# A perceiver block on one core: the last group's self attention on float32 weights, and Mamba's buffers handed to the last stage

## The chip, the cores and the metric

The kernel runs on one core of a Trainium2 chip. The metric is the device time of one execution in microseconds; lower is better. A kernel's time is the median of several executions, and one more execution is recorded with the hardware profiler.

## The reference, cut to what matters

Eight batches of 64 query rows (512 wide) pass through six residual layers. The change touches layer 5, and its buffers touch layer 2.

```python
x = x + xattn0(layernorm(x), ctx, ...)   # cross attention, 32 heads, 1601 context rows
x = x + mamba(layernorm(x), ...)         # selective scan, 1024 channels x 16 states
x = x + ternary_ffn(layernorm(x), ...)
x = x + xattn1(layernorm(x), ctx)        # attention on the raw context, no weights
x = x + attention_fwd(layernorm(x), wq, wk, wv, wo)   # causal, 32 heads of 16
x = x + octonion_ffn(layernorm(x), w_gate, w_up, w_down)

def attention_fwd(x, wq, wk, wv, wo):
    xq, xk, xv = heads(x @ wq.T), heads(x @ wk.T), heads(x @ wv.T)   # 512 x 512 each
    xq, xk = rotary(xq), rotary(xk)
    probs = softmax(where(causal, xq . xk * 0.25, -1e30))
    return (probs . xv) @ wo.T
```

## The kernel before, in words

The first cross attention is the long part: for each batch and each of eight KV heads it projects keys and values, scores, exponentiates and sums. The layers after it work on a "group" of two batches, 128 rows, in a generator called `chain`. There are four groups. The chains of the first three are drawn out under the cross attention of later batches: `advance` takes steps from them by a clock of planned costs (`SPAN`, `CHAIN_COST`). When the last batch's cross attention is done, the fourth chain starts with nothing left to hide under, and the third chain is not yet finished. From about 2430 us to the end these two chains run side by side. In this text they are the **third group** and the **last group**. The order of the instructions on each engine is fixed when the program is built, by a scheduler that works with planned times; on the chip every engine takes its instructions in that order.

Weights come from DRAM at every use. A weight product goes through `mm3`: the left side and the weight are each held as a high and a low float32r part, and three matmuls (high x high, high x low, low x high) make one product of 128 x 512. The parts of the four 512 x 512 attention weights are made once, early, by `prep`, and kept in DRAM as `wat_s` (the profile's `d_wat`); the float32 originals are the input `attnT`. Where a weight is exact in one part (`exact=True`: the ternary layers, `d_ffn`, `d_gu`, `d_dn`), two matmuls are enough.

All loads are issued by one queue, SP's, in program order, so a load that waits for its buffer holds those behind it. Buffers are taken from pools by tag, with a number of slots for each tag:

- The last group draws from the pool `tp` with `BUFS_TAIL`: `s4` (slots of 4 KB in each partition) holds Mamba's inputs and scan tiles, the high and low weight pair of an `mm3` (tile `s`), the context tiles of the second cross attention and the gate and up weights `gu`; `w2` (slots of 2 KB, 12 of them, tile `w`) holds Mamba's projection weights, the ternary weights and the down weights `dn`.
- The third group holds its weights in tile `w_r`: 4 slots of 2 KB, `REST = {"w2": 4}`. Its attention loads high and low parts one by one.
- The first three groups have one pool, `cp`, for all other tiles, Mamba's among them (`a2`, `lv`, `bc`, `xpad`, `sm`).

In the last group's `attn1`, the projections for K, Q and V come in this order, then scores and values for four blocks of eight heads (`scores`, `values`), and the output product `wo` block by block. `ffn1` follows with an order of its own (`FFN_TAIL`): `lins` (gate and up, matmuls of L1200, one block of 48), `act` and `down`. In the third group `ffn1` takes its steps one after another: for each of three column ranges (512, 512, 336) gate, up, `act`, `down`. It has two PSUM buffers, and `dn` keeps one of them to the end. The lines of the steps: L740, L742 and L743 are the three matmuls of `mm3`; L699 transposes a normalised row block, L1095 a rotated K or Q, L1152 the probabilities, L1223 the input of `down`; L1118 puts the causal mask into PSUM (a float32 matmul), L1125 scores, L1159 values; L101 and L102 make the high and low part of a left side; L1086 is the rotation's first step; L1204 takes gate or up out of PSUM; L714 to L717 with L127 to L130 are the silu; L1235 is the last addition, L771 stores the output.

Of the kernel before, what the change touches and what calls it, by code (L numbers as in the profile page):

```python
# [9 lines left out]
FR = mybir.dt.float32r  # L10
# [6 lines left out]
P = 128  # L17
D = 512
NC = 4
# [21 lines left out]
AVPLAN = ((), (), (0, 1, 2, 3), (4, 5, 6, 7), (8, 9, 10, 11), (12,))  # L41
EXPLAN = ((0,), (1, 2), (3,), (4, 5), (6,), ())
BUFS = {"a2": 4, "lv": 3, "bc": 1, "xpad": 1, "b2": 5, "b4": 2, "w2": 3, "xr": 2}
BUFS_TAIL = {"a2": 6, "du": 2, "bc": 2, "xpad": 4, "s4": 10, "kb": 3, "b2": 8, "b4": 3, "w2": 12, "xr": 2}

# [28 lines left out]
class Kernel:  # L76
# [11 lines left out]

    def sb(self, tag, shape, dt=FP, bufs=None, pool=None):
        if pool is None:  # L90
            pool, bufs = self.cp, bufs or self.bufs.get(tag)
            if tag in REST and self.tp and not self.tail:
                pool, bufs, tag = self.tp, REST[tag], tag + "_r"
        return pool.tile(shape, dt, name=self.nm(tag), tag=tag, bufs=bufs)
# [624 lines left out]
    def lin(self, lt, wts, N=D, exact=False, tg="w2"):  # L719
# [3 lines left out]
            self.mm3(ps, lambda a: lt(c, a), w, N, c == 0, c == len(wts) - 1, exact, tg)  # L723
        return ps

    def mm3(self, ps, lhsT, wt, N, start, stop, exact=False, tg="w2"):

        nc = self.nc
        if exact:
            wh = self.sb(tg, [P, D], FR)[:, :N]  # L730
            nc.sync.dma_start(out=wh.bitcast(FP), in_=wt)
        elif self.tail:
            w = self.sb(tg, [P, 2, D], FR)
            nc.sync.dma_start(out=w.bitcast(FP), in_=wt)
            wh, wl = w[:, 0], w[:, 1]
        else:
            wh, wl = (self.sb(tg, [P, D], FR) for _ in range(2))
            nc.sync.dma_start(out=wh.bitcast(FP), in_=wt[:, 0])
            nc.sync.dma_start(out=wl.bitcast(FP), in_=wt[:, 1])
        nc.tensor.matmul(ps, lhsT=lhsT(0), rhs=wh, start=start, stop=False)  # L740
        if not exact:
            nc.tensor.matmul(ps, lhsT=lhsT(0), rhs=wl, start=False, stop=False)  # L742
        nc.tensor.matmul(ps, lhsT=lhsT(1), rhs=wh, start=False, stop=stop)  # L743
# [334 lines left out]

    def attn1(self, x, xo):
        nc = self.nc  # L1080
        lt = self.lnT(x, P)
        tr = []
        for m in (1, 0):
            ps = self.lin(lt, self.wat_s[m], tg=self.t4)
            t1 = self.sb("b2", [P, D])
            nc.scalar.activation(t1, ps, AF.Copy, scale=self.rot[:, 0:1])  # L1086
            r = self.sb("b2", [P, D])
            psv = ps.rearrange("p (d two) -> p d two", two=2)
            tv = t1.rearrange("p (d two) -> p d two", two=2)
            rv = r.rearrange("p (d two) -> p d two", two=2)  # L1090
            nc.vector.scalar_tensor_tensor(rv[:, :, 0], psv[:, :, 1], self.rot[:, 1:2], tv[:, :, 0], ALU.mult, ALU.add)
            nc.vector.scalar_tensor_tensor(rv[:, :, 1], psv[:, :, 0], self.rot[:, 2:3], tv[:, :, 1], ALU.mult, ALU.add)
            tp = self.acc().rearrange("p (c t) -> p c t", t=P)
            for c in range(NC):
                nc.tensor.transpose(tp[:, c, :], r[:, c * P : (c + 1) * P], self.ident)  # L1095
            t = self.sb(self.tl, [P, NC, P])
            nc.scalar.copy(t, tp)
            tr.append(t)
            yield 4
        kT, qT = tr  # L1100
        ps = self.lin(lt, self.wat_s[2], tg=self.t4)

        vb = self.sb("b4", [P, 16, 2, 32])
        nc.gpsimd.memset(vb, 0.0)
# [4 lines left out]
                    ps[k * T : (k + 1) * T].rearrange("p (hp h2 d) -> p hp h2 d", h2=2, d=16)[:, :, h2, :],  # L1109
                )  # L1110
        yield 4
        ot = self.sb("b4", [P, 2, NC, P], FR)

        def scores(c):
            sp = self.acc()
# [31 lines left out]
        def values(c, s):  # L1147

            tp = self.acc().rearrange("p (k q) -> p k q", q=P)
            sf = s.rearrange("p h t -> p (h t)")  # L1150
            for k in range(NC):
                nc.tensor.transpose(tp[:, k, :], sf[:, k * P : (k + 1) * P], self.ident)  # L1152
            pT = self.sb("b2", [P, NC, P])
            nc.scalar.copy(pT, tp)
            op = self.acc()
            for b in range(2):
                cols = slice(b * T, (b + 1) * T)
                for k in range(NC):
                    nc.tensor.matmul(op[k * 32 : (k + 1) * 32, cols], lhsT=vb[:, c * NC + k, b, :], rhs=pT[:, k, cols], start=True, stop=True)  # L1159
            self.split(ot[:, 0, c], ot[:, 1, c], op[:, :P])  # L1160

        def wo(c):
            self.mm3(ps, lambda a: ot[:, a, c], self.wat_s[3][c], D, c == 0, c == NC - 1, tg=self.t4)

        ahead = self.ahead
        ss = []
        for c in range(NC + ahead):
# [3 lines left out]
            if c >= ahead:  # L1171
                values(c - ahead, ss[c - ahead])
                yield 3
                if self.tail:
                    if c == ahead:
                        ps = self.acc()
# [64 lines left out]
    def run(self):  # L1241
        nc, tc, ctx = self.nc, self.tc, self.ctx
        nc.scalar.preload_act_table_set("natural_log_exp_and_others")
        self.setup(bufs=BUFS, accb=2, hs=4, tail=False, ahead=1, **TAGS)
        self.pc = ctx.enter_context(tc.tile_pool(name="pc", bufs=2, space=PSUM))
        xctx = ctx.enter_context(ExitStack())
        self.px = xctx.enter_context(tc.tile_pool(name="px", bufs=2, space=PSUM))
        self.consts()
        self.scratch()
        self.xw = ctx.enter_context(tc.tile_pool(name="xw", bufs=2))  # L1250
        self.xp = xctx.enter_context(tc.tile_pool(name="xp", bufs=2))
        qctx = ctx.enter_context(ExitStack())
        self.q_ln(qctx.enter_context(tc.tile_pool(name="qp", bufs=2, side="right")))
        B = self.B
        sizes = GROUPS.get(B) or [1] * B
        groups, k = [], 0
        for m in sizes:
            groups.append(list(range(k, k + m)))
            k += m
        self.place = {b: (k * T, len(g) * T) for g in groups for k, b in enumerate(g)}  # L1260
        side, self.tp = [], None

        def start(gen, now, cost, end):
            env = {k: getattr(self, k) for k in ENV}
            if not self.tail:
                env["nc"] = Side(self, PINNED)
            side.append({"gen": gen, "cost": cost, "got": 0.0, "t0": now, "end": end, "env": env})

        def advance(now):
            base = {k: getattr(self, k, None) for k in ENV}  # L1270
            for c in list(side):
                self.setup(**c["env"])
                goal = c["cost"] * min(1.0, (now - c["t0"]) / max(c["end"] - c["t0"], 1e-9))
                if now >= c["end"]:
                    goal = 1e9
                while c["got"] < goal:
                    try:
                        c["got"] += next(c["gen"])
                    except StopIteration:
                        if PRINT_COST:  # L1280
                            print("side", c["got"])
                        side.remove(c)
                        break
            self.setup(**base)

        gi, now, xdone = 0, 0.0, 0.0
        for cost, fin in self.x_all(list(range(B))):
            xdone += cost
            advance(xdone / X_COST)
            if fin == 0:  # L1290
                qctx.close()
                self.cp = ctx.enter_context(tc.tile_pool(name="cp", bufs=2, side="right"))
                start(self.prep(), xdone / X_COST, PREP_COST, PREP_END)
            if fin is not None and gi < len(groups) and groups[gi][-1] == fin:
                g = groups[gi]
                now = xdone / X_COST
                last = gi == len(groups) - 1
                if last:
                    self.pinning = False
                    xctx.close()  # L1300
                    self.pc = ctx.enter_context(tc.tile_pool(name="pt", bufs=3, space=PSUM))
                    self.cp = self.tp = ctx.enter_context(tc.tile_pool(name="tp", bufs=2))
                    self.setup(bufs=BUFS_TAIL, accb=6, hs=8, tail=True, ahead=2, **TAGS_TAIL)
                start(self.chain(gi, g), now, CHAIN_COST, now + SPAN[gi])
                if last:
                    side.insert(0, side.pop())
                gi += 1
        while side:
            now += 0.01
            advance(now)  # L1310
# [1 line left out]

TAGS = {"tw": "a2", "ts": "a2", "td": "a2", "tc4": "b4", "tk": "b2", "t4": "w2", "tl": "b2", "tn": "w2", "tv": "lv"}
TAGS_TAIL = {"tw": "w2", "ts": "s4", "td": "s4", "tc4": "s4", "tk": "kb", "t4": "s4", "tl": "s4", "tn": "w2", "tv": "s4"}
ENV = ("nc", "cp", "pc", "bufs", "accb", "hs", "tail", "ahead", *TAGS)
GROUPS = {8: [2, 2, 2, 2], 2: [2]}
SPAN = [3.1,3.1,2.6,0.2]
PREP_END = 2.8
FFN_TAIL = (("l", 0), ("l", 1), ("a", 0), ("l", 2), ("a", 1), ("d", 0), ("a", 2), ("d", 1), ("d", 2))
REST = {"w2":4}  # L1320
OTB = 1
SPV, HV = 2, 1
X_COST = 236.0
# [112 lines left out]
```

## Time and profile before

| | |
|---|---|
| median of 3 executions | 2746.58 us (2745.26 to 2748.1) |
| profiled execution: device time | 2747.45 us |
| profiled execution: span of the trace | 2745.6 us |
| instructions | 47783 |
| third group's Mamba layer done (last L743 on tile `a`) | about 2400 us |
| third and last group alone on the core | about 2430 to 2745.6 us |
| HBM traffic | 384.42 MB read, 72.48 MB written |

The profiled execution is 1.85 us longer than its span, which is what lies around the trace, and 0.87 us above the median.

How to read the views: the page gives busy time by engine and, in 40 slices of 68.6 us, the busy share in tenths. The chain of waits follows the work that ended last back to what released it; each line has start, length in us, and what it was: an engine's instruction, or a DMA waited for. The timeline lists the instructions of an engine in order of time; a bracket gives the idle time before one and what ended it. SPq is the DMA queue; its lines give when loads were issued. Instructions named f32 on TensorE include float32r; a true float32 matmul shows as two instructions.

### The profile page before, as it was taken

Reading aid. Unit: us, or ns where it says so; the run is one execution under the profiler, and the core shown is the slowest. Engines: PE = TensorE matmul, PEld = TensorE weight load, DVE = VectorE, ACT = ScalarE, POOL = GpSimd, SP = SyncE. Lnnn points to the kernel's source line nnn. Section 1 sums busy time; section 2 is a strip of 40 time slices with the busy share of each in tenths; the row PEclk is TensorE's granted clock in tenths of the full one; section 3 lists DMA queues with packets and bytes.
Section 4 is the critical chain, followed back from the end, with each engine's and each line's share of the span. In section 5 each row is a group of like instructions: output and inputs, shape, how many; then the busy total and the mean of one; then the engine's idle time right before and its main releaser. Section 6 shows DMA issues by size and latency. Waiting matters only on the chain.

```text
span 2745.6 us, 47783 instructions
## 1 busy us (share of the span) xinstructions
PE 2584.6 (94%) x17840; PEld 2303.7 (84%) x17840; DVE 1756.7 (64%) x2988; ACT 1378.4 (50%) x3318; POOL 1163.1 (42%) x1175
## 2 busy tenths in 40 slices
PE   7999999999999899999999989999999999976778
PEld 6999999889889899978988988988897998954545
DVE  4544345577777886545587787454668787549645
ACT  4444555444556554544456555444556555435433
POOL 3212444474579653421367344421348435215220
PEclk9999999999999999999999999999999999978889
DMA  9544446664666234664325534665333543465676
GB/s 305 151 144 152 131 155 221 204 205 156 212 208 212 71 116 164 215 192 155 114 78 156 156 106 131 199 203 165 125 101 97 168 153 126 146 221 197 219 253 218
DMA packets 312167, 460.03 MB, mean 168 GB/s; under 512 B 81272, under 2 KB 188792, under 8 KB 307456
## 3 DMA queue, kind: packets, MB, share of 16 engines
q1 hardware_dynamic: 311936, 456.99, 51.6%
q8 instruction: 140, 2.29, 0.3%
q14 instruction: 91, 0.75, 0.1%
HBM read 384.42 MB, written 72.48 MB: 166 GB/s over the span
## 4 chain that ended last, share of the span: by engine, by line
PE 60%; DVE 15%; DMA 9%; POOL 7%; issue 5%; ACT 4%; SPq 1%; POOLq 0%; DVEq 0%; ACTq 0%
PE v_ps L325 14%; PE k_ps L354 13%; PE o_ps L438 8%; PE s_ps L374 7%; DVE a L62 4%; PE w_ps L495 3%; POOL a L62 3%; PE acc L270 2%; POOL ss L426 2%; PE acc L1000 2%; PE acc L1053 2%; PE acc L740 2%; DMA cst<-in_ctxT_dram 2%; PE acc L743 1%; PE acc L785 1%
## 5 line engine op out<-in xcount | busy, mean ns | idle before, releaser
L354 PE MATMUL k_ps<-cxb,wk 128*128 128x256 f32 x3840 | 560.9, 291 | 21.8 <-ACT cxb L101 9.6
L354 PEld LDWEIGHTS k_ps<-cxb,wk 128*128 128x128 f32 x3840 | 504.9, 191 | 55.8 <-issue 15.1
L325 PE MATMUL v_ps<-wv,cxb 128*128 128x256 f32 x3840 | 521.5, 283 | 7.4 <-DVE mx L381 3.3
L325 PEld LDWEIGHTS v_ps<-wv,cxb 128*128 128x128 f32 x3840 | 479.2, 189 | 28.2 <-issue 13.9
L374 PE MATMUL s_ps<-q,kt 128*128 128x256 f32 (+1 forms) x2496 | 414.9, 299 | 13.3 <-DVE kt L105 4.9
L438 PE MATMUL o_ps<-S,v 128*128 128x256 f32 (+1 forms) x1664 | 409.2, 380 | 1.7 <-ACT S L416 1.6
L374 PEld LDWEIGHTS s_ps<-q,kt 128*128 128x128 f32 (+1 forms) x2496 | 339.7, 185 | 38.0 <-DVE kt L105 7.2
L381 DVE TENSOR_TENSOR mx<-s_ps,mx 128x512 f32<-128x512 f32 x256 | 175.3, 685 | 306.5 <-ACT S L377 306.3
L426 POOL TENSOR_TENSOR ss<-ss,S 128x512 f32<-128x512 f32 x256 | 355.0, 1387 | 16.2 <-ACT S L416 1.5
L377 ACT COPY S<-s_ps 128x512 f32<-128x512 f32 (+1 forms) x448 | 241.5, 551 | 211.8 <-PE s_ps L374 210.7
L438 PEld LDWEIGHTS o_ps<-S,v 128*128 128x128 f32 (+1 forms) x1664 | 296.4, 190 | 33.9 <-ACT S L416 2.5
L418 POOL TENSOR_TENSOR ss<-S,S 128x512 f32<-128x512 f32 x64 | 84.2, 1316 | 566.2 <-ACT S L416 566.0
L104 ACT ACTIVATE kt<-k_ps,c_bk 128x256 fp32r<-128x256 f32 (+1 forms) x384 | 184.7, 481 | 220.1 <-PE k_ps L354 216.1
L105 DVE SCALAR_TENSOR_TENSOR kt<-k_ps,c_bk,kt 128x256 fp32r<-128x256 f32 (+1 forms) x384 | 187.7, 489 | 144.0 <-ACT kt L104 143.2
L415 DVE TENSOR_TENSOR S<-S,m_ps 128x512 f32<-128x512 f32 (+1 forms) x448 | 257.6, 641 | 28.6 <-PE m_ps L401 27.6
L416 ACT ACTIVATE S<-S 128x512 f32<-128x512 f32 (+1 forms) x448 | 247.2, 599 | 42.5 <-DVE S L415 41.9
L328 ACT COPY v<-v_ps 128x256 f32<-128x256 f32 (+1 forms) x416 | 152.3, 367 | 219.6 <-PE v_ps L325 217.9
L62 ACT ACTIVATE a<-lv,c_A_log 128x128 f32<-128x128 f32 x384 | 122.7, 392 | 126.6 <-DVE lv L62 120.3
L62 POOL TENSOR_TENSOR a<-bc,lv 128x512 f32<-128x512 f32 x96 | 128.2, 1336 | 127.7 <-DVE a L62 112.4
L102 POOL TENSOR_TENSOR cxb<-cst,cxb 128x256 fp32r<-128x256 f32 x160 | 126.3, 804 | 120.9 <-ACT cxb L101 118.0
L62 DVE TENSOR_TENSOR_SCAN a<-a,a 128x512 f32<-128x512 f32 x96 | 145.1, 1512 | 48.3 <-POOL a L62 47.9
L325 PE MATMUL v_ps<-wv,cxt 128*128 128x256 f32 (+1 forms) x1152 | 161.8, 286 | 2.2 <-DVE kt L105 2.2
(348 smaller groups left out, 3972.0 us busy)
## 6 DMA issues: line engine op xcount, KB each, us to landing
wo<-d_wo SPq DMA_DIRECT2D x96, 512.0 KB, 4.9
wk<-d_wk SPq DMA_DIRECT2D x63, 512.0 KB, 3.4
wv<-d_wv SPq DMA_DIRECT2D x31, 1024.0 KB, 7.0
cst<-in_ctxT_dram SPq DMA_DIRECT2D x160, 128.0 KB, 3.1
b<-in_ctxN_dram SPq DMA_DIRECT2D x36, 512.0 KB, 4.2
d_q<-q_t SPq DMA_DIRECT2D x32, 512.0 KB, 4.3
q<-d_q SPq DMA_DIRECT2D x64, 256.0 KB, 3.6
d_wo<-b SPq DMA_DIRECT2D x32, 512.0 KB, 2.9
```

The source lines that it names most:

```text
L62: return lambda *a, **k: self.tc.keep_in_program_order(f(*a, **k))
L104: nc.scalar.activation(hi, src, AF.Identity, bias=bias)
L105: eng.scalar_tensor_tensor(lo, src, bias, hi.bitcast(FP), ALU.add, ALU.subtract)
L325: nc.tensor.matmul(ps[:r], lhsT=cx[:, a, c, o : o + r], rhs=w[:, m, c, :], start=k == 0, stop=k == 11)
L354: nc.tensor.matmul(ps[:, :wd], lhsT=w[:, a, c, :], rhs=cx[:, m, c, :], start=k == 0, stop=k == 11)
L374: nc.tensor.matmul(sp[:r, gi, :], lhsT=kt[:, a, u * P : u * P + r], rhs=q[:, m, :], start=k == 0, stop=k == 2)
L377: nc.scalar.copy(s[:r, :n], sp[:r, :n])
L381: nc.vector.tensor_tensor(mx, sp, S[0] if len(S) == 1 else mx, ALU.max)
L415: nc.vector.tensor_tensor(sv, sv, ps[:r, 1:2].to_broadcast([r, w, 256]), ALU.add)
L416: nc.scalar.activation(sv, sv, AF.Exp, scale=ISC)
L426: nc.gpsimd.tensor_tensor(ss, ss, S[n], ALU.add)
L438: nc.tensor.matmul(ps[:, 0], lhsT=self.v[(b, j, t)][:r, hc : hc + P], rhs=S[t // 2][:r, t % 2], start=t == 0, stop=t == NT - 1)
```

## The change

1. In the last group, `attn1` takes its left sides as one float32 tile (`lnT` with `hl=False`, `ot` without a low part) and its weights as float32 from `attnT`, in a new function `mm32`: one load of 256 KB into a slot of `w2` and one float32 matmul for each product, in place of one load of 512 KB into a slot of `s4` and three float32r matmuls. There are 16 such products: K, Q, V and `wo`, four each.
2. Mamba's tags move from `cp` to a pool `ca` of their own, stacked on `cp`. When the last group starts, `ca` is closed together with the cross attention's pool, and `tp` may use its memory.
3. `s4` gets 16 slots in place of 10.

The third group's attention stays as it is.

```diff
-BUFS_TAIL = {"a2": 6, "du": 2, "bc": 2, "xpad": 4, "s4": 10, "kb": 3, "b2": 8, "b4": 3, "w2": 12, "xr": 2}
+BUFS_TAIL = {"a2": 6, "du": 2, "bc": 2, "xpad": 4, "s4": 16, "kb": 3, "b2": 8, "b4": 3, "w2": 12, "xr": 2}
...
-            pool, bufs = self.cp, bufs or self.bufs.get(tag)
+            pool, bufs = self.ca if tag in MAMBA_TAGS else self.cp, bufs or self.bufs.get(tag)
...
+    def mm32(self, ps, x, wt, start, stop):
+
+        w = self.sb("w2", [P, D])
+        self.nc.sync.dma_start(out=w, in_=wt)
+        self.nc.tensor.matmul(ps, lhsT=x, rhs=w, start=start, stop=stop)
...
     def attn1(self, x, xo):
         nc = self.nc
-        lt = self.lnT(x, P)
+        tail = self.tail
+        lt = self.lnT(x, P, hl=not tail)
+        w32 = self.i["attnT"]
+
+        def proj(m):
+            if not tail:
+                return self.lin(lt, self.wat_s[m], tg=self.t4)
+            ps = self.acc()
+            for c in range(NC):
+                self.mm32(ps, lt(c, 0), w32[m, c], c == 0, c == NC - 1)
+            return ps
...
-        ot = self.sb("b4", [P, 2, NC, P], FR)
+        ot = self.sb("b4", [P, 1, NC, P]) if tail else self.sb("b4", [P, 2, NC, P], FR)
...
-            self.split(ot[:, 0, c], ot[:, 1, c], op[:, :P])
+            if tail:
+                nc.scalar.copy(ot[:, 0, c], op[:, :P])
+            else:
+                self.split(ot[:, 0, c], ot[:, 1, c], op[:, :P])
...
+            if tail:
+                self.mm32(ps, ot[:, 0, c], w32[3, c], c == 0, c == NC - 1)
+            else:
+                self.mm3(ps, lambda a: ot[:, a, c], self.wat_s[3][c], D, c == 0, c == NC - 1, tg=self.t4)
...
+                actx = ctx.enter_context(ExitStack())
+                self.ca = actx.enter_context(tc.tile_pool(name="ca", bufs=2, side="right"))
...
                     xctx.close()
+                    actx.close()
...
-                    self.cp = self.tp = ctx.enter_context(tc.tile_pool(name="tp", bufs=2))
+                    self.ca = self.cp = self.tp = ctx.enter_context(tc.tile_pool(name="tp", bufs=2))
...
+MAMBA_TAGS = ("a2", "lv", "bc", "xpad", "sm")
```

More of the change, by code (lines that the diff above doesn't have):

```diff
@@ L1080, in attn1 @@
         nc = self.nc
-        lt = self.lnT(x, P)
+        tail = self.tail
[8 more added lines that the diff above has]
+            return ps
         tr = []
         for m in (1, 0):
-            ps = self.lin(lt, self.wat_s[m], tg=self.t4)
+            ps = proj(m)
             t1 = self.sb("b2", [P, D])
@@ L1100, in attn1 @@
         kT, qT = tr
-        ps = self.lin(lt, self.wat_s[2], tg=self.t4)
+        ps = proj(2)
         vb = self.sb("b4", [P, 16, 2, 32])
@@ L1159, in values @@
                     nc.tensor.matmul(op[k * 32 : (k + 1) * 32, cols], lhsT=vb[:, c * NC + k, b, :], rhs=pT[:, k, cols], start=True, stop=True)
-            self.split(ot[:, 0, c], ot[:, 1, c], op[:, :P])
+            if tail:
+                nc.scalar.copy(ot[:, 0, c], op[:, :P])
+            else:
+                self.split(ot[:, 0, c], ot[:, 1, c], op[:, :P])
         def wo(c):
-            self.mm3(ps, lambda a: ot[:, a, c], self.wat_s[3][c], D, c == 0, c == NC - 1, tg=self.t4)
+            if tail:
+                self.mm32(ps, ot[:, 0, c], w32[3, c], c == 0, c == NC - 1)
+            else:
+                self.mm3(ps, lambda a: ot[:, a, c], self.wat_s[3][c], D, c == 0, c == NC - 1, tg=self.t4)
         ahead = self.ahead
@@ L1314 @@
 TAGS_TAIL = {"tw": "w2", "ts": "s4", "td": "s4", "tc4": "s4", "tk": "kb", "t4": "s4", "tl": "s4", "tn": "w2", "tv": "s4"}
-ENV = ("nc", "cp", "pc", "bufs", "accb", "hs", "tail", "ahead", *TAGS)
+ENV = ("nc", "cp", "ca", "pc", "bufs", "accb", "hs", "tail", "ahead", *TAGS)
 GROUPS = {8: [2, 2, 2, 2], 2: [2]}
```

## The prediction

> **What bounds the kernel now.** First the page, for the place. TensorE is busy 94% of the span at a full clock; the last five slices (2402 us on) are another regime: PE falls to 6 or 7 tenths, the clock to 7 or 8, DMA rises to 7.
>
> ```profile
> PE   7999999999999899999999989999999999976778
> PEclk9999999999999999999999999999999999978889
> DMA  9544446664666234664325534665333543465676
> ```
>
> Only there does the change act: no engine's order differs before the last group's Mamba scans. So next the chain of waits from 2640 us (start, length, what).
>
> ```profile
> 2655.25 5.94 DMA s<-d_wat
> ...
> 2661.24 0.79 PE acc L740
> 2662.03 0.43 PE acc L742
> ...
> 2672.29 5.37 DMA s<-d_wat
> ...
> 2679.36 1.71 PE acc L1118 x2
> ...
> 2694.44 0.86 PE acc L1118 x2
> ...
> 2709.97 8.96 PE acc L1200 x31
> ```
>
> The last group's Q and V weights arrive late (5.94 and 5.37 us), and after each wait TensorE runs at half clock: a 128x512 float32r matmul takes 0.43 us, later 0.23; the float32 mask matmul 1.71, later 0.86. Then comes the block of L1200. Last, the timeline of TensorE after it: the third group ends the kernel, not the last group.
>
> ```profile
> 2721.52 0.60 PE L1223 MATMUL acc<-ident,b 128*128 128x128 f32 x4
> 2723.77 0.49 PE L740 MATMUL acc<-w_r,b 128*128 128x512 f32 x1 [1.65 <-ACT b L101]
> ...
> 2727.63 0.39 PE L740 MATMUL acc<-w_r,b 128*128 128x336 f32 x1 [1.12 <-DMA w_r<-d_gu]
> ...
> 2739.83 0.49 PE L740 MATMUL acc<-w_r,b 128*128 128x512 f32 x1 [0.57 <-ACT b L101]
> ```
>
> These are the third group's second down-projection (to 2726.5), its last gate and up (to 2733.4) and its third down-projection (to 2741.9). Both groups finish within 3 us of each other, so a gain for one is worth only what the other allows.
>
> **What the Trainium skill says.** "TensorE: Matmul & The Clock Gate", What's actually happening: the clock is half after an idle window of about 3.4 us, full after as long a busy one. The trace agrees: 0.43 against 0.23 us. The same page's opening table calls the queues of ScalarE and VectorE strict FIFO; agrees: at 2578.74 ScalarE did the third group's L1086 (0.69 us) before the last Mamba cast L101 at 2579.32, which TensorE waited for. "FP8 and Floating Point Precision", TensorE Precision Notes: true FP32 takes four passes; agrees: 0.86 is 3.7 times 0.23. "DMA: Bandwidth & Descriptors", Anatomy of one DMA, gives 2.0 us plus bytes at 436 GB/s for GpSimd's path, an estimate of 2.6 us for 256 KB; SP's loads of that size, four alone at 2648.5, had a median of 2.5 us, the fourth 3.95.
>
> **The change part by part**, set against the span (2745.6).
>
> *Costed at nothing.* The pools: the third group's Mamba is done at 2400, and `tp`'s first load waits for the cross attention's pool anyway (issued 2429.72). Should `ca` be freed late, that load and all behind it on SP move by as much. Mamba with 16 slots: SP waited 19.3 + 6.2 us at L734 for slots, and these waits shrink, but VectorE is busy 48.4 of 50 us in 2500 to 2550, so the scans set the pace. The down weights: eleven loads of 256 KB stood before attention in the queue or within it; eight `attnT` loads of the same size take eight of those places, and `dn` follows the attention's weights. Its cover is the whole score stage, over 20 us. Traffic falls by 16 x 0.26 = 4.2 MB, 14 us of DMA at the 300 GB/s of 2650 to 2710; after 2710 DMA is 34% busy, so this shortens waits only where I count them below.
>
> *To the last group's K* (2649.5 before). Taken: 2.5 us earlier. The Mamba cast now stands ahead of L1086 and the third group's matmuls around it come later (2 us at the last L743), and the left side has no low part (L102, 0.7). Against it, eleven context loads now stand in SP's queue ahead of the third group's K weights c2 and c3, and those matmuls stand in TensorE's order ahead of the last Mamba L743; Q c2, loaded behind four `attnT` loads, stands ahead of the last group's scores. Bounds: 5 us earlier, 6 later. K starts at 2647.
>
> *K to the L1200 block* (60.5 us before: 2649.5 to 2709.97).
> - The weight waits go: 5.9 + 5.4. The slow matmuls behind them go: eleven float32r by 0.20, three by 0.20, L1118 and the scores after it by 1.8, together 4.6. Two waits for `w_r` on a loaded DMA (0.5 each) go. Sum -16.9.
> - Sixteen products: 0.86 for 3 x 0.23: +2.7. Four passes aside, K starts after 7 us with little work, so two of its matmuls at half clock: +1.7.
> - TensorE's new order: two of the third group's `wo` products (0.7 each) move behind K, +1.4; 16 of its gate and up matmuls leave, 16 x 0.23 = -3.7; scores of blocks 1 and 2 lose their overlapped partner, a lone one taking 1.0 us, +1.5; its first gate matmul stands between these scores and must wait until L102 frees one of two PSUM buffers, +1.5.
> - VectorE's new order puts the third group's silu (L715, L129, L130, L717, four times 0.7) between the steps of the layer norm ahead of the block: +2.8.
>
> Sum 51.5, so the block starts at 2698.5. It takes its 11.5 us as before (the idle stretch before it, and so the half clock, is alike) and ends at 2710.0, **11.5 us earlier** than 2721.5.
>
> *After the block* (24.1 us before). Here the third group has more left. Before, its second gate and up came before the block; now they follow it. Gate: weights there, 8 x 0.23 = 1.9. Up: its four loads take the slots that gate frees; SP issues 0.55 apart, the fourth lands 3.95 later: done at +6.1. Then the order has two of the last group's down-projections (transposes 0.6, cast 0.58, subtraction 0.69, hops, eight matmuls 1.9) and only then the transposes of the third group's second one. These wait for its silu, and VectorE has 11 us of work from +7 on: two silus of the last group, one of the third (3.6), two subtractions. Transposes at +17.5, second down-projection done at +21.9 with 14 matmuls shared. From there as before (2726.5 to 2745.6): four slots, two rounds of loads, silu, last down-projection, 19.1. Sum 41.0, which is 16.9 more than before.
>
> The end is at 2710.0 + 41.0 = 2751.0; some 40 hops of 0.02 to 0.05 us ("issue" in the chain) are not in the sum, +1. So 2752.0, **6.4 us more** than 2745.6. Against the median 2746.58, which stands 0.87 below the profiled 2747.45: **2753 us**.
>
> **The rivals.** The forecast's own range is 2748 to 2760.
> (a) *The saved waits carry through.* For it: 11.3 us of waits on the chain are certain to go, and with the clock kept full and the silu clear of the layer norm the block would end at 2704 (less 1.7, 2.8 and 1.5). If what follows then costs 33.5 us (24.1 as before, 6.1 for gate and up, 3.3 for the down-projections between), the end is 2737.5 on the span's clock, against the median 2738.5. Against it: four slots, one load round each 4 us. It decides as soon as the block ends more than 17 us earlier, or what follows costs under 5 us more than before.
> (b) *A head-of-queue wait on the way to K.* The eleven context loads are 5.4 MB; at 330 GB/s 16 us. If they are not landed by 2578, the third group's K c2 holds the last Mamba product and all behind it: 4 to 10 us, 2760 with the rest as forecast. For it: SP's in-order queue. Against: DMA runs at 133 GB/s in 2560 to 2570, so there is room.
> (c) *Gain and loss cancel.* If the terms of order (+1.5, +1.5, +2.8) hide beside other work, the end is 2747.
> That the change does not do what it says is excluded: the built order shows 16 loads from `attnT` and 16 single products on `w`.
>
> **How the numbers follow.** A measurement here can tell about 0.2% (5.5 us: 2741.1 to 2752.1) from no change. Forecast 0.53, of which 0.16 falls below 2752.1; (a) 0.22, nearly all faster; (b) 0.12, slower; (c) 0.13, same. Faster 0.21, same 0.30, slower 0.49. For 8 in 10, leaving out half of (a)'s lower side and (b)'s upper end: 2738 to 2766.
>
> **What would show it.** Right: no wait for `d_wat` by the last group; the L1200 block ends 9 to 14 us earlier; at the end SP issues some 26 `w_r` loads in rounds of four, and the last group's store stands well before the third's. Wrong: a block that ends under 6 us earlier (the terms of order or (b) are larger), or a third group whose last gate starts before 2725 (then (a)).

## The result and the profile after

The changed kernel takes 2764.59 us (median of 4, 2761.38 to 2772.36), the kernel before 2745.92 in the same comparison: ratio 1.0064, 95% interval 1.0049 to 1.008. The profiled execution took 2765.68 us, its span 2763.8, which is 18.2 more than before.

The page first: engine and DMA rows by slice.

```profile
PE   7999999999999899999999989999999999977886
PEclk9999999999999999999999999999999999977898
DMA  9544446664665244764325533655323553375753
```

The last five slices are again the only odd ones (TensorE 7, 7, 8, 8, 6 tenths where it was 7, 6, 7, 7, 8). The chain of waits from 2575 us (start, length, what), of the changed kernel:

```profile
2586.03 5.42 DMA w_r<-d_wat
...
2659.86 4.84 PE acc L730 x8
...
2667.08 3.45 PE acc L730 x8
...
2672.86 3.44 PE acc L730 x8
...
2711.10 9.90 PE acc L1223 x48
2721.50 3.33 DMA w_r<-d_gu
...
2742.90 3.48 DMA w_r<-d_gu
```

K, Q and V of the last group (L730, three times eight instructions, two to a float32 product) no longer wait for weights; 3.44 us for eight is 0.86 for a product, and K's 4.84 holds the slow clock. Both waits for `d_wat` are gone. The block (L1223, L1200 before) ends at 2721.0, where it ended at 2721.7 before: by the two traces' own clocks 0.7 us is left of what was saved (how much of that is scatter follows below). And after it come two waits for the third group's weights. TensorE's timeline there (a bracket is the idle time and what ended it):

```profile
2724.96 0.47 PE L746 MATMUL acc<-w_r,b 128*128 128x512 f32 x1 [2.10 <-DMA w_r<-d_gu]
...
2742.51 0.39 PE L749 MATMUL acc<-w_r,b 128*128 128x512 f32 x1
2743.94 0.39 PE L746 MATMUL acc<-w_r,b 128*128 128x336 f32 x1 [1.04 <-DMA w_r<-d_gu]
...
2755.51 0.88 PE L1246 MATMUL acc<-ident,b 128*128 128x128 f32 x3 [4.66 <-DVE b L1236]
```

These are the third group's second up projection, the last product of its second down-projection, its last gate, and the transposes of its third down-projection, which wait 4.66 us for its silu. The store of the last group's output is issued at 2742.4, the third's at 2760.9.

So that runs can be compared, the time is cut into stages, each read from the timelines: the end of the cross attention's output (L495, nothing of the change acts ahead of it); from there to the last group's K; K to the block; the block; and what follows it. "Scans" is from the first to the last of the last group's scan instructions on VectorE and lies within the second stage. "Behind" is the number of the third group's matmuls on `w_r` that the built order puts after the block. All in us, one profiled execution each; the last column is the ratio of the times to those of the kernel before in the same comparison, with its interval.

| kernel | cross ends | (scans) | to K | K to block | block | after | behind | ratio |
|---|---|---|---|---|---|---|---|---|
| before | 2429.7 | 89.3 | 219.9 | 60.5 | 11.7 | 23.9 | 30 | 1 |
| changed | 2435.2 | 93.3 | 224.5 | 51.3 | 10.1 | 42.8 | 46 | 1.0064 (1.0049 to 1.008) |
| e1 changed again | 2428.6 | 94.3 | 224.0 | 53.7 | 10.1 | 43.3 | 46 | 1.0057 (1.004 to 1.0073) |
| e2 float32 only | 2431.1 | 89.8 | 218.6 | 51.8 | 10.5 | 38.0 | 38 | 1.0022 (1.0012 to 1.0032) |
| e3 float32, pools | 2427.9 | 90.8 | 219.7 | 51.8 | 10.5 | 38.0 | 38 | 1.0015 (1.0 to 1.003) |
| e4 pools, 16 slots | 2428.9 | 93.6 | 220.8 | 56.5 | 11.7 | 45.2 | 46 | 1.0073 (1.0054 to 1.0092) |
| e5 slots of the scans | 2428.4 | 91.8 | 220.7 | 53.4 | 10.1 | 42.6 | 46 | 1.0046 (1.0031 to 1.0061) |
| e6 float32, third early | 2447.2 | 93.1 | 216.8 | 47.3 | 10.1 | 20.2 | 0 | 0.9987 (0.9977 to 0.9997) |
| e7 third early | 2447.4 | 92.4 | 213.0 | 49.6 | 12.1 | 21.1 | 6 | 0.9997 (0.9987 to 1.0007) |
| e8 all, third early | 2447.7 | 95.1 | 214.0 | 53.8 | 10.1 | 19.5 | 0 | 1.0 (0.9988 to 1.0011) |
| e9 order kept | 2435.0 | 91.4 | 224.2 | 56.5 | 10.3 | 23.8 | 30 | 0.9992 (0.9984 to 1.0) |
| e10 16 slots, early | 2448.2 | 91.5 | 213.7 | 50.8 | 10.1 | 19.3 | 0 | 0.9982 (0.9973 to 0.9991) |
| e11 six slots | 2429.3 | 90.9 | 215.2 | 53.8 | 10.1 | 39.0 | 42 | 1.0004 (0.9993 to 1.0014) |
| e12 eight slots | 2434.5 | 92.0 | 213.6 | 53.3 | 10.1 | 21.0 | 6 | 0.9941 (0.9927 to 0.9955) |

Of the 18.2 us between the first two profiled executions, 5.5 lie ahead of all that was changed. The rest, 12.7 with rounding, is +4.6 to K, -9.2 from K to the block, -1.6 in the block, +18.9 after it.

### The profile page after: what moved, and what is told of

The parts are those of the page before. It is cut to its first block, busy times and chain, and to the rows that moved or that the text cites. A ratio compares the mean times of both kernels' runs of the same rounds, so it can differ in the third digit from the quotient of the medians.

```text
span 2763.8 us, 47736 instructions
## 1 busy us (share of the span) xinstructions
PE 2601.4 (94%) x17824; PEld 2307.3 (83%) x17824; DVE 1758.4 (64%) x2983; ACT 1380.8 (50%) x3318; POOL 1163.3 (42%) x1175
## 4 chain that ended last, share of the span: by engine, by line
PE 61%; DVE 14%; DMA 9%; POOL 8%; issue 5%; ACT 4%; SPq 1%; POOLq 0%; DVEq 0%; ACTq 0%
PE v_ps L325 14%; PE k_ps L354 13%; PE o_ps L438 8%; PE s_ps L374 7%; DVE a L62 4%; DMA cst<-in_ctxT_dram 3%; PE w_ps L495 3%; PE acc L270 3%; POOL a L62 2%; POOL ss L426 2%; PE acc L746 2%; PE acc L791 2%; PE acc L1006 2%; PE acc L749 2%; PE acc L1059 2%
## 5 line engine op out<-in xcount | busy, mean ns | idle before, releaser
L374 PEld LDWEIGHTS s_ps<-q,kt 128*128 128x128 f32 (+1 forms) x2496 | 338.8, 185 | 40.0 <-DVE kt L105 10.5
L62 DVE TENSOR_TENSOR_SCAN a<-a,a 128x512 f32<-128x512 f32 x96 | 147.7, 1539 | 47.7 <-POOL a L62 47.3
```

The lines of the kernel that those rows point to most:

```text
L62: return lambda *a, **k: self.tc.keep_in_program_order(f(*a, **k))
L374: nc.tensor.matmul(sp[:r, gi, :], lhsT=kt[:, a, u * P : u * P + r], rhs=q[:, m, :], start=k == 0, stop=k == 2)
```

## The experiments

**e1, the changed kernel again.**

> The changed kernel once more, for a second trace. In the first one 5.6 us of the 18.2 us were there when the cross attention's output ended (2435.2 against 2429.7 us), before any work that the change moves. If that is scatter of one execution, the cross attention ends this time anywhere in 2429 to 2436. If the split of the pools (other addresses for Mamba's tiles from 330 us on) causes it, it ends at 2434 to 2436 again. The stage of the last group's scans (first scan to the end of the last) took 93.3 us against 89.3: if GpSimd's multiplications holding up VectorE's causes that, it is 92.5 to 94 again, with VectorE's 256-element products of two SBUF tensors at up to 1.5 us. Time 2759 to 2766 in all theories.

2765.29 us. The cross attention ended at 2428.6, 6.6 earlier than in the first trace: the 5.5 us ahead of the tail were scatter of one execution, and the kernel before itself ran from 2742 to 2760 us in this comparison. The scan stage is long again, 94.3.

Why it is long is seen where the same VectorE instructions stand in both kernels. They belong to the last group's own Mamba layer: a silu of its gate (L715, L129, L717; 256 wide only in the last group). First VectorE before, then GpSimd before, around them (start, length, engine, line, operation):

```profile
2510.36 0.40 DVE L717 TENSOR_TENSOR s<-s,a 128x256 f32<-128x256 f32 x1
...
2512.07 0.41 DVE L129 TENSOR_TENSOR a<-a,a 128x256 f32<-128x256 f32 x1
2512.41 0.28 DVE L715 TENSOR_SCALAR a<-a 128x256 f32<-128x256 f32 x1
```

```profile
2508.29 0.73 POOL L970 TENSOR_TENSOR a<-a,a 128x256 f32<-128x256 f32 x1
2518.37 2.67 POOL L916 TENSOR_TENSOR s<-bc,du 128x512 f32<-128x512 f32 x2 [9.35 <-PE acc L920]
```

The same of the changed kernel, VectorE and then GpSimd:

```profile
2516.53 1.05 DVE L717 TENSOR_TENSOR s<-s,a 128x256 f32<-128x256 f32 x1
2517.50 0.68 DVE L924 TENSOR_TENSOR s<-acc,bc 128x512 f32<-128x512 f32 x1
2518.10 0.75 DVE L907 TENSOR_TENSOR s<-s,s 128x128 f32<-128x128 f32 x1
2518.78 1.49 DVE L129 TENSOR_TENSOR a<-a,a 128x256 f32<-128x256 f32 x1
...
2523.06 1.35 DVE L715 TENSOR_SCALAR a<-a 128x256 f32<-128x256 f32 x1
```

```profile
2516.03 8.23 POOL L922 TENSOR_TENSOR s<-bc,du 128x512 f32<-128x512 f32 x6
```

Before, GpSimd sat idle for 9.35 us until TensorE freed a slot of `s4`, and in that time VectorE's silu took 0.40, 0.41 and 0.28. With 16 slots GpSimd runs six products back to back, and the same instructions take 1.05, 1.49 and 1.35; taken singly, each ends 0.1 to 0.3 us after one of GpSimd's six does. The instruction with one input in PSUM and one in SBUF (L924, 0.68) is not touched. This is what the Trainium skill, "SBUF - State Buffer", Who interferes with whom, states: a VectorE instruction with two SBUF inputs, or one in a two-port mode (it names `tensor_scalar`), and a GpSimd instruction that reads SBUF lock each other out for a whole instruction, while one with a single SBUF input outside those modes goes on. The trace agrees, in GpSimd's median too: 1.27 us for L916 before, 1.44 for L922. Summed over VectorE's 47 instructions of the scan stage that use only the SBUF tiles `a` and `s`: 22.7 us before, 27.6 and 28.6 in the two traces of the changed kernel. That is the whole of the loss in this stage: VectorE runs the same 138 instructions in it, in another order, and its idle time falls from 2.3 to 1.8 us. Long ones stand in the kernel before too (up to 1.48 us), but 3 of the 47 are over 1 us there, and 10 and 11 in the changed kernel.

**e2, float32 attention alone, and e3, the same with the split pools.** e2 takes `self.cp` for all tags:

```diff
-"s4": 16
+"s4": 10
-            pool, bufs = self.ca if tag in MAMBA_TAGS else self.cp, bufs or self.bufs.get(tag)
+            pool, bufs = self.cp, bufs or self.bufs.get(tag)
```

> Float32 attention alone: one pool and 10 slots of s4 as before. Slot theory (16 slots let GpSimd run its multiplications without pauses and hold up VectorE's): the scan stage returns to 89 to 90.5 us, the rest of the changed kernel stays (K to the block of the down-projection 51, after the block 42), time 2750 to 2759. Order theory (the float32 attention shifts the third group's work into the scan stage, slots don't matter): scan stage 93 to 94, time 2759 to 2766. Pool theory (the split of the pools makes everything ahead of 2430 us slower): cross attention ends at 2429 to 2431, time 5 us below the changed kernel.

> Float32 attention with the split pools, but 10 slots of s4. Every engine's order is that of float32 alone with one pool; only addresses and what a pool waits for differ. Slot theory and scatter: the same time as float32 alone within 2 us. Pool theory: cross attention ends at 2434 to 2436, time 5 us above float32 alone.

2755.68 and 2754.44 us, where before is 2749.29. With 10 slots the scan stage is 89.8 and 90.8 and the 47 instructions take 22.8 and 23.4, in the order of the kernel before: the slots, with the order that they bring, make the stage long, and float32 does not. The split of the pools costs nothing that can be told. Float32 alone loses 4 to 6 us: it saves 8.7 from K to the block, and pays 14.1 after it (the stage took 38.0 us, where 42 were expected), where 38 products of the third group now stand in place of 30.

**e4, pools and 16 slots, high and low weights as before.** The edit is in `attn1`.

```diff
-        tail = self.tail
+        tail = False
```

> Split pools and 16 slots of s4 alone; the last group's attention keeps its high and low float32r weights and three products. Slot theory: scan stage 92 to 94 us as in the changed kernel; against it the weights of Q and V may be loaded earlier into the free slots, so that of the two waits of 5.9 and 5.4 us some goes: 2742 to 2752. Order theory: scan stage 89 to 90.5, time 2738 to 2747. Pool theory: cross attention ends at 2434 to 2436, time 2748 to 2755.

2768.08 us, above every bound given; the whole change took 2765.29 in the same comparison, and the two intervals overlap. The scan stage (93.6) is as the slot theory has it. What no theory had is the time after the block: 45.2. The chain of waits of e4:

```profile
2670.17 5.39 DMA s<-d_wat
...
2706.12 11.71 PE acc L1223 x48
...
2719.54 3.58 DMA w_r<-d_gu
...
2740.87 3.82 DMA w_r<-d_gu
```

The slots alone make the planner put 46 of the third group's products behind the block, with their two waits for `w_r`, although nothing of the third group was edited. One wait for the last group's weights stays on the chain (5.39), but TensorE itself stood idle for those weights for only 0.3 and 0.5 us.

**e5, slots of their own for the scans** (in `BUFS_TAIL` and `TAGS_TAIL`; `h8` is the new tag of the scans' products).

```diff
-"s4": 16        "ts": "s4"
+"s4": 13, "h8": 3   "ts": "h8"
```

> The changed kernel, but the scans' GpSimd products get three slots of a tag of their own, and s4 keeps 13 of its 16: GpSimd can run at most three tiles ahead again, all else may still be loaded early. 46 products of the third group still stand after the block of the last group's gate and up. Pacing theory (GpSimd running ahead locks VectorE out): scan stage 89 to 91 us in place of 93.3 and 94.3, VectorE's two-input products there at 23 us in place of 28, time 3 to 5 us below the changed kernel, which is 2760 to 2762 where that is 2765. Rival (the scan stage is longer because of the order of work): 93 to 94.5, 2764 to 2766.

2762.71 us, ratio 1.0046. GpSimd pauses again (its timeline in e5):

```profile
2515.39 2.68 POOL L922 TENSOR_TENSOR h<-bc,du 128x512 f32<-128x512 f32 x2 [7.01 <-PE acc L926]
2523.58 2.50 POOL L922 TENSOR_TENSOR h<-bc,du 128x512 f32<-128x512 f32 x2 [5.51 <-PE acc L926]
```

The stage up to K is 220.7, 3.3 to 3.8 below the changed kernel, the time after the block unchanged (42.6). The scan stage itself fell to 91.8, just above the 89 to 91 expected. The instructions got short again (23.9 us for the 45 of them in this order's scan stage, GpSimd's median 1.27), but VectorE now stands idle for 5.0 us of the stage, where it was 1.8: holding GpSimd back has a price of its own. By the intervals the gain in time, about 0.1 to 0.2%, is not clear of the scatter; the stage times carry the reading.

**e6 to e8, the third group's due time** (the third entry of `SPAN`, by which the planner spreads the group's steps). With 2.65 the planner puts all or nearly all of the third group ahead of the block; e6 is e2 with it, e7 the kernel before, e8 the whole change.

```diff
-SPAN = [3.1,3.1,2.6,0.2]
+SPAN = [3.1,3.1,2.65,0.2]
```

> Float32 attention alone (one pool, 10 slots), and the third group's due time set from 2.60 to 2.65, which makes the planner put all of its work ahead of the last block of the last group: no product of it stands after the block (38 with float32 alone, 30 in the kernel before). Theory (float32 saves 8 to 9 us from K to the block, and the third group's work behind the block eats them): after the block 20 to 25 us in place of 38, time 2735 to 2745 where before is 2749. Rival (the third group's work costs as much ahead of the block): block later by 10 to 14, time 2750 to 2756.

> The kernel before with the same due time, 2.65: control for the order alone, with high and low weights and their waits. 6 products of the third group stand after the block. Theory: float32 is worth 5 to 10 us when nothing behind the block eats it, so this one lands 5 to 10 us above the float32 kernel with that due time: 2743 to 2752. Rival (the order is all): within 2 us of it.

> The whole change with the due time 2.65: no product of the third group after the block. What 16 slots cost beside float32 alone was 10 us: 4 to 5 in the scan stage, the rest behind the scans. Theory: the second part comes from the third group's products put behind the block and goes here, so this one lands 4 to 6 us above the float32 kernel with 2.65. Rival (the slots delay something else behind the scans): 9 to 12 above it.

2745.46, 2747.88 and 2749.94 us, where before is 2749.89. After the block all three take 19.5 to 21.1, but the cross attention ends at 2447, where it was 2428 to 2435: the third group's work has gone to where it holds up the cross attention. e6 so misses its theory's 2735 to 2745, if barely, and neither it nor the rival foresaw where the cost would go. Float32 is worth 2.4 us here (e7 less e6), not the 5 to 10 of the theory, and with intervals that overlap it is not clearly more than nothing. In the traces it saves 2.2 from K to the block, 2.1 in the block and 1.0 after it, and loses 3.8 ahead of K. The 16 slots cost 4.5 (e8 less e6; these intervals overlap a little too), the number expected, but not at the place expected: the scans are 2.0 longer, yet the stage to K is 2.8 shorter, and K to the block is 6.5 longer.

**e9, the order kept.** Three own slots for the scans and 9 of `s4`; by chance of the planner the sequence after the block is that of the kernel before.

```diff
-"s4": 16        "ts": "s4"
+"s4": 9, "h8": 3    "ts": "h8"
```

> Float32 attention and split pools, three slots of their own for the scans' GpSimd products and 9 for s4, due times as before. In this division the planner leaves 30 products of the third group after the block, in the same sequence as in the kernel before (46 in the changed kernel, 38 with float32 and 10 slots). Theory (float32 saves 8 to 9 us from K to the block and 1.2 in the block; what is lost is lost only by the products put behind it and by GpSimd running ahead): K to the block 51 to 53 us, block 10 to 10.5, after the block 24 to 27, time 6 to 10 us below the kernel before. Rival (the waits return in another place whatever the order): within 3 us of it.

2747.99 us, ratio 0.9992: the rival's size. After the block (23.8, where the theory had 24 to 27) and block (10.3) are near enough as the theory said, K to the block is not: 56.5. The chain of e9 ahead of the block:

```profile
2702.04 3.53 DMA w_r<-d_gu
...
2709.45 3.05 DMA w_r<-d_gu
2715.69 7.44 PE acc L1223 x31
```

Waits for the third group's four slots that the changed kernel has behind the block now stand ahead of it: TensorE's own waits for `w_r` are 2.3 us ahead and 1.4 behind, in the changed kernel's first trace none ahead and 4.7 behind, in the kernel before 2.6 and 1.1. Moving its products across the block moves much of their cost. The forecast's saving shrinks with them: with 46 matmuls on `w_r` between K and the block, as before, that stage is 4.0 us shorter than before; in the changed kernel, where 36 stand there, it is 7 to 9 shorter. Read so, part of that saving was work put behind the block. The stage to K also came out 4.3 longer than before, 2.1 of it in the scans; the rest was not taken apart.

**e10, float32 with 4 own slots, 12 of `s4` and the due time 2.65.**

> Float32 attention, split pools, four own slots for the scans' GpSimd products and 12 for s4, the third group's due time 2.65: none of its products after the block. Theory: scan stage 91 to 93 us in place of the 95.1 of the whole change with 2.65, so 2 to 4 us below that kernel, 0 to 2 below float32 with 2.65 (2743 to 2748 where before is 2749). Rival (the third group's work ahead of the block sets the time, not the scans): as the whole change with 2.65, equal to before.

2746.34 us where before is 2750.34, ratio 0.9982. The scan stage is 91.5 against e8's 95.1, the time about 5 us (0.0018) below e8's ratio and 1.4 below e6's; e8's interval and e10's still overlap, e6's and e10's almost coincide. And the 3.6 us do not reach K: cross attention to K is 213.7 against 214.0. What e10 gains over e8 is read from K to the block (50.8 against 53.8).

**e11, six slots for the third group, and e12, eight.** e11 is the changed kernel with one number altered; e12 also has 4 own slots for the scans and 10 of `s4`, so that it fits.

```diff
-REST = {"w2":4}
+REST = {"w2":6}
```

> The changed kernel with six slots in place of four for the third group's weights; 42 of its products after the block in place of 46. Theory of the prediction (rounds of four loads set the time after the block): the waits for these loads after the block, 4.7 us on TensorE, fall to 1 to 3, after the block 38 to 41 us in place of 42.8 and 43.3, time 2 to 5 us below the changed kernel. Rival (the silu and the sharing of VectorE set it): after the block 42 to 44, same time within 2 us.

2751.15 us: 0.5 to 0.6% below the changed kernel, where 2 to 5 us were expected. The expected part is there: 39.0 after the block, and TensorE has no wait for `w_r<-d_gu` left behind K. The larger part was not foreseen: K comes 9 us sooner after the cross attention, 4.7 of it ahead of the first scan, 2.4 in the scans, 2.2 behind them. No matmul on `w_r` stands on TensorE between the cross attention's end and the last scans in either kernel, so the first part is no wait of TensorE for these slots; the built order on VectorE differs from 2452 us on, and whether that or the loads in SP's queue brought it was not taken apart. The scan stage is a limit to the reading of e2 to e5: here it takes 90.9 us with 16 slots, its 47 instructions 25.5. How long VectorE's instructions get hangs on which of them the order puts beside GpSimd's, not on the slots alone.

```diff
-REST = {"w2":4}   "s4": 16              "ts": "s4"
+REST = {"w2":8}   "s4": 10, "h8": 4     "ts": "h8"
```

> Float32 attention and split pools, eight slots for the third group's weights in place of four, four own slots for the scans' products and 10 for s4 in the memory given up; due times as before. 6 products of the third group stand after the block, and nothing differs ahead of the last group's tail, so the cross attention's output ends at 2428 to 2436 (with the due time 2.65 it ended at 2447). Theory (the third group's four slots and their rounds of loads set both the stretch ahead of the last group's K and the time after the block): from the cross attention's end to K 212 to 217 us, K to the block 50 to 54, after the block 20 to 24, time 2728 to 2740, 10 to 20 below the kernel before. Rival (what leaves the time after the block comes back ahead of it, as with the order kept): K to the block 58 to 65, time 2744 to 2750.

2734.21 us where before is 2748.62: ratio 0.9941 (0.9927 to 0.9955), faster than both kernels. Every stage lies within what its theory gave. The due time is the old one, and with it the cross attention ends where it did (2434.5); with eight slots the built order still puts only 6 products behind the block. K comes 213.6 us after the cross attention, and the gain ahead of it lies behind the scans: 66.4 us from the last scan to K, where it was 74.5. The end of TensorE's timeline in e12:

```profile
2701.37 10.09 PE L1223 MATMUL acc<-s,b 128*128 128x512 f32 x48
2711.29 0.49 PE L1246 MATMUL acc<-ident,b 128*128 128x128 f32 x3
2712.91 0.50 PE L746 MATMUL acc<-w_r,b 128*128 128x512 f32 x1 [1.13 <-ACT b L101]
...
2717.32 1.12 PE L1246 MATMUL acc<-ident,b 128*128 128x128 f32 x4 [2.38 <-DVE b L1236]
```

Of the third group only its last down-projection stands after the block, and no load of it is issued there. Slots and order changed together in e12, and eight slots with the high and low weights were not run, so how much of the 14 us is the slots', and how much needs float32, stays open.

## Why the prediction fell short

The direction held: slower, by 6.4 us to 2753 in the forecast, by 18.7 to 2764.6 as measured. The size fell short: 2764.6 lies above the forecast's own 2748 to 2760, and the wide range, to 2766, holds it by 1.4 us. That was luck, since the only reason given for a time above 2760 was rival (b), whose wait did not come. Counted from the end of the cross attention, which no change touches, before takes 316.0 and the changed kernel 328.6 and 331.1: 12.6 and 15.1 more.

One reading behind the forecast has to be put right first: the two waits for `d_wat`, 5.94 and 5.37 us on the chain of waits, were not both TensorE's. On TensorE before, most of the first stood under a wait for the third group's layer norm:

```profile
2659.37 1.08 PE L699 MATMUL acc<-ident,b 128*128 128x128 f32 x4 [4.32 <-DVE b L140]
2661.24 0.79 PE L740 MATMUL acc<-s,b 128*128 128x512 f32 x1 [0.78 <-DMA s<-d_wat]
...
2677.71 0.79 PE L740 MATMUL acc<-s,b 128*128 128x512 f32 x1 [5.38 <-DMA s<-d_wat]
```

So TensorE waited 6.2 us for the weights, not 11.3, and the 4.3 for the layer norm went with the new order. It stood idle for 15.2 us from K to the block before, for 7.3 and 8.7 after.

- **K to the block, 60.5 to 51.5:** measured 51.3 and 53.7. The two waits went and K's slow products cost 1.4 (4.84 less 3.44; 1.7 forecast). The sum came out near by luck, the terms did not: in place of 2.8 and 1.5 between the layer norm and the scores there is one wait of 5.35 us, at 2705.75, of the third group's transposes for its silu, ahead of the block.
- **The block, 11.5 "as before":** 10.1. Eight products of the third group stand between that wait and the block and take the slow clock on themselves (0.79 us each at first, 0.40 at the end).
- **After the block, 41.0:** 42.8 and 43.3. Up projection done at +6.6 (6.1 forecast), second down-projection at +21.9 (21.9), the rest 20.9 (19.1), where the silu holds the last transposes. SP issues 23 loads of `w_r` from 2709 us on, in rounds of four (26 forecast); e11 shows that four slots are part of it.
- **To K, 2.5 us earlier: the step that failed.** It came 4.6 and 4.1 later, so the block ended 6.2 us earlier counted from the cross attention's end (0.7 by the traces' clocks), and 4.3 in the second trace, not 9 to 14. Under 6 was the prediction's own sign of being wrong. Scans to K is unchanged (74.5 before, 74.2 and 72.9), so neither the gain of 2.5 was there, nor rival (b)'s wait. The scan stage is what grew, by 4.0 and 5.1. Its step is among those **costed at nothing**: "VectorE is busy 48.4 of 50 us in 2500 to 2550, so the scans set the pace". That VectorE was full was right, and was the reason to worry: GpSimd, freed of its wait for slots and in the order that 16 slots bring, makes VectorE's own instructions longer (4.9 and 5.9 us in sum). The cover was itself what got slower. By the first trace this term is off by 7.1 us; the others together by less than 1.
- **Six slots of `s4` more, costed at nothing, in the order:** the forecast took the built order as one thing. e2 and e4 show that the slots alone bring the third group's products behind the block (46, against 38 with float32 alone and 30 before), and that they, not float32, bring most of the loss: 0.73% without float32, and with it 0.57 against 0.22%.
- **The pools, at nothing:** right (e2 and e3).
- **Rival (a)** failed at both points that it named itself: the block did not end 17 us earlier, and what follows it cost 19 us more, not under 5. **Rival (c)** failed too: the terms of order did not hide, and the end is far above 2747.
- The profiled 18.2 us hold 5.5 of scatter. The prediction set its sum against one execution, whose early part alone can be off by 7.

## What to carry to other kernels

More buffers for a producer are not free when it is GpSimd: where VectorE set the pace and worked from SBUF beside it, letting GpSimd run ahead lengthened VectorE's instructions (47 of them from 22.7 us to 27.6); GpSimd's pauses for a slot in the kernel before cost little and kept VectorE fast. Where two chains end side by side, a saving in one is worth what the other allows: here the third group decided. Float32 in the last group alone lost time (e2), and with more slots for the third group, and the order that came of them, the same float32 is part of a kernel that is 0.6% faster (e12). And a change in buffer counts moves the order of work that nobody edited, so count what stands behind the last block in the built order before and after.

## What was not expected of the hardware

A 128x256 VectorE instruction of 0.40 us takes up to 1.49 beside GpSimd's products, and GpSimd's median of 1.27 becomes 1.44: both lose. Executions of one kernel scatter by more than most of the tail's effects: before ran from 2741 to 2760 us over all comparisons, and the stretch ahead of the tail, with the same work in the same order, ended between 2427.9 and 2435.2 us.
